# Layer 1 of a two-layer graph network: sums and masks accumulated onto a relu in PSUM, two heads each for VectorE and GpSimd

## The chip, the cores and the metric

The kernel runs on one core of a Trainium2 chip. A core has five engines that work through their own instruction queues and wait for one another by semaphores: TensorE (PE in the profile, with its weight loads as PEld), VectorE (DVE), ScalarE (ACT), GpSimd (POOL) and SyncE (SP), which here only issues DMAs. TensorE writes its results to PSUM, which has eight banks of 128 x 512 float32[...]. The metric is the device time of one execution in microseconds; lower is better.

## The reference

Two layers over 4096 nodes with 512 features. Layer 0 is an attention in which the dense matrix adj is added to the scores. Layer 1, where the change lies, is a graph attention with 8 heads of 64 features. Cut to what matters:

```
h  = relu(layernorm(x))
nX = per-head normalised (h @ W), 8 heads x 64
at1[k,i], at2[k,j] = nX . a1, nX . a2              # per head k
kg[k,i,j] = leaky_relu(at1[k,i] + at2[k,j], 0.2) * adj[i,j]
mg = where(adj[i,j] != 0, kg, -32768)
y  = softmax_j(mg) @ nX + nX
x  = x + elu(y)
```

So each of the 8 x 4096 x 4096 logits is a sum of two vectors, bent at zero, multiplied by adj, masked, and put through an exponential; the row sums of the softmax come out of the product with nX through a column of ones.

## The kernel before

Layer 0 prepares, beside its own work, what layer 1 reads: adj transposed with a tiny value in place of the zeros (gT_d, float32), a mask that is 0 or a huge negative number (nT_d, bfloat16), and the vectors at1 and at2, each split into three bfloat16 parts (z1_d, z2_d), so that a product over six rows gives their exact sum.

Layer 1 is a loop over 512 steps. A step (ic, hg, jt) has 512 target columns (GC), four heads (HG) and 128 source rows. 32 steps (NB, over jt) make a group, which has one pair of accumulators; there are 16 groups, of 8 column chunks with two halves of the heads each. Every instruction goes through seq, so each engine runs its instructions in the order in which the program writes them, which is the order of the loop's body.

With leaky_relu(s) = 0.2 s + 0.8 max(s, 0), the four logits of a step are formed in two ways.

- The left two heads (0 and 1). z_sums makes, on TensorE, 0.2 s in PSUM (line 970, "6*128": a product over six rows) and adds the mask to it with the identity (line 978, eight products of 64 x 64 blocks a step over nb and nx, the mask and its halves swapped). ScalarE's relu (line 986) reads the same PSUM and writes relu(4 z) to SBUF as t; VectorE adds the two (line 1002).
- The right two heads (2 and 3). TensorE makes only at1's part and the mask; VectorE adds the larger of two vectors to it (line 996, one instruction for each head), which is the same function.

Then all four heads are multiplied by adj (g). In an ordinary step VectorE multiplies head 3 from PSUM (line 1001) and GpSimd the other three in SBUF (line 1009, 128x1536). In four "light" steps of each 32 (jt 11, 17, 23, 29) VectorE takes two heads and GpSimd two. ScalarE's exponential (line 1012, 128x2048) and TensorE's product with nX into the accumulators acc (line 1025) follow, three and four steps later.

PSUM has three buffers "d" of two banks, which the left pair, the right pair and small tiles of other work share, and the two accumulators: eight banks. t has six buffers in SBUF. Each step's body issues, in this order: values(n-4), exponent(n-3), leaky(n) with VectorE's work, weigh(n) on GpSimd, z_sums(n+1), relu(n+1). load_adj brings, with SP's queue, the next four steps' masks and g, into two buffers each.

When a group ends, finish spreads its rest over the next 17 steps, by the dictionary later: ScalarE copies the accumulators (copies, line 1041), TensorE turns them (to_rows, line 1047, into a "d" buffer), VectorE divides (lines 1056 and 1057), DMAs on POOL's queue add rows in DRAM (add, line 1063: nX's own rows at step 3, y at 11, x at 14), and ScalarE computes the elu with five kinds of activation (lines 1072 to 1082), before close writes out. The first layer-1 group also runs make_ready for the last rows of layer 0, whose small PSUM tiles use "d".

Of the kernel before, what the change touches and what calls it, by code (L numbers as in the profile page):

```python
# [10 lines left out]
F32 = mybir.dt.float32  # L11
BF16 = mybir.dt.bfloat16
AF = mybir.ActivationFunctionType
# [5 lines left out]
P = 128  # L19
# [59 lines left out]
def fast_path(  # L79
# [817 lines left out]
    with tc.tile_pool(name="ga_in", bufs=2) as inputs, tc.tile_pool(  # L897
# [5 lines left out]
        STEPS = [(ic, hg, jt) for ic in range(NI) for hg in range(NH // HG) for jt in range(NB)]  # L903
        n_steps = len(STEPS)
        inverses = gat.tile([P, NI, 2, 2, 2, 4], F32, name="inverses")
        inverses = gat.tile([P, NI, 2, 2, 2, 4], F32, name="inverses")
        loads, logits, zs, groups = {}, {}, {}, {}

        light = {n for n in range(n_steps) if n % NB in (11, 17, 23, 29)}
        later = {}  # L910

        def load_adj(q):
# [45 lines left out]
                for f in range(2)  # L958
            ]

        def z_sums(n):

            ic, hg, jt = STEPS[n]
            _, masks, z2 = loads[n // JB]
            pair = [None, None]
            for hf in (1, 0):
                pair[hf] = psum.tile([P, 2, GC], F32, name="d", tag="d", bufs=3)
            for hh in (2, 3, 0, 1):
                rows = slice(32 * hh, 32 * hh + 6)
                seq(nc.tensor.matmul(  # L970
                    pair[hh // 2][:, hh % 2, :], z2[rows, ts(jt % JB, P)],
                    groups[ic, hg]["z1"][rows, :], start=True, stop=False,
                ))

            for first in (2, 0):
                for r, c in ((0, 0), (1, 1), (0, 1), (1, 0)):
                    hh, rows = first + r, ts(r, HD)
                    seq(nc.tensor.matmul(  # L978
                        pair[hh // 2][ts(c, HD), hh % 2, :], ident_b[rows, rows],
                        masks[r != c][rows, jt % JB, :], start=False, stop=True,  # L980
                    ))
            zs[n] = pair

        def relu(n):
            t = work.tile([P, HG, GC], F32, name="t", tag="t", bufs=6)
            seq(nc.scalar.activation(t[:, 0:2, :], zs[n][0], AF.Relu, scale=4.0))  # L986
            logits[n] = t

        def leaky(n):

            ic, hg, jt = STEPS[n]
            t, pair, u4 = logits[n], zs.pop(n), groups[ic, hg]["u4"]
            mine = 2 if n in light else 1
            for e in (1, 0):
                h = hg * HG + 2 + e
                seq(nc.vector.scalar_tensor_tensor(  # L996
                    pair[1][:, e, :] if e > 1 - mine else t[:, 2, :], u4[:, e, :],
                    at2m[:, jt, h : h + 1], pair[1][:, e, :], ALU.max, ALU.add,
                ))
            g = loads[n // JB][0][:, jt % JB, :].unsqueeze(1).to_broadcast([P, mine, GC])  # L1000
            seq(nc.vector.tensor_mul(t[:, HG - mine : HG, :], pair[1][:, 2 - mine : 2, :], g))  # L1001
            seq(nc.vector.tensor_add(t[:, 0:2, :], t[:, 0:2, :], pair[0]))  # L1002

        def weigh(n):

            mine = 2 if n in light else 3
            g = loads[n // JB][0][:, STEPS[n][2] % JB, :].unsqueeze(1).to_broadcast([P, mine, GC])
            t = logits[n]
            seq(nc.gpsimd.tensor_mul(t[:, 0:mine, :], t[:, 0:mine, :], g))  # L1009

        def exponent(n):
            seq(nc.scalar.activation(logits[n], logits[n], AF.Exp))  # L1012

        def values(n):

            ic, hg, jt = STEPS[n]
            grp = groups[ic, hg]
            if jt == 0:
                grp["acc"] = [
                    psum.tile([P, GC], F32, name=f"acc{hf}", tag=f"acc{hf}", bufs=1) for hf in range(2)  # L1020
                ]
            t = logits.pop(n)
            for hf in range(2):
                for e in range(2):
                    seq(nc.tensor.matmul(  # L1025
                        grp["acc"][hf][ts(e, HD), :], nX[jt // SB][:, jt % SB, hg * HG + 2 * hf + e, :],
                        t[:, 2 * hf + e, :], start=jt == 0, stop=jt == NB - 1,
                    ))

        def finish(n, ic, hg):  # L1030

# [8 lines left out]
                for hf in range(2):  # L1040
                    seq(nc.scalar.copy(ob[:, hf, :], grp["acc"][hf]))

            def to_rows(hf):
                pt = psum.tile([P, 2, GC], F32, name="pt1", tag="d", bufs=3)
                for b in range(SB):
                    col = (b % 2) * 2 * HB
                    seq(nc.tensor.matmul(  # L1047
                        pt[:, b // 2, col : col + 2 * HB], ob[:, hf, ts(b, P)],
                        back.rearrange("p e c -> p (e c)"), start=True, stop=True,
                    ))  # L1050
                grp["pt"] = pt[:, :, 0 : 4 * HB].rearrange("p k (q c) -> p k q c", c=HB)

            def divide(hf):
                v = grp.pop("pt")
                rinv = inverses[:, ic, hg, hf]
                seq(nc.vector.reciprocal(rinv, v[:, :, :, HD]))
                seq(nc.vector.tensor_mul(  # L1057
                    y[:, hf].rearrange("p (k q) e -> p k q e", k=2), v[:, :, :, 0:HD],
                    rinv.unsqueeze(3).to_broadcast([P, 2, 4, HD]),
                ))  # L1060

            def add(t, what):
                seq(nc.gpsimd.dma_start(out=flat(t), in_=what, accum_op=ALU.add))

            def of_group(ap):
                return ap[ic, hg].rearrange("p f b d -> p (f b d)")

            def flat(t):
                return t.rearrange("p f q e -> p (f q e)")

            def minus(hf):
                seq(nc.scalar.activation(grp["e"][:, hf], y[:, hf], AF.Relu, scale=-1.0))

            def exps(hf):
                e = grp["e"][:, hf]
                seq(nc.scalar.activation(e, e, AF.Exp, scale=-1.0))  # L1076

            def positive():
                seq(nc.scalar.activation(flat(y), flat(y), AF.Relu))  # L1079

            def less_one():
                seq(nc.scalar.add(flat(grp["e"]), flat(grp["e"]), -1.0))

            def close():
                e = grp["e"]
# [5 lines left out]
            if n > n_steps:  # L1091
# [25 lines left out]
                        in_=e[:, hf].rearrange("p (b h) e -> p b (h e)", h=2),  # L1117
                    )
                return
            for d, place, f in (  # L1120
                (0, "mid", copies),
                (1, "mid", lambda: to_rows(0)), (1, "end", lambda: divide(0)),
                (2, "mid", lambda: to_rows(1)), (2, "end", lambda: divide(1)),
                (3, "end", lambda: add(y, of_group(own_d))),
                (6, "end", room), (6, "end", lambda: minus(0)), (7, "end", lambda: minus(1)),
                (8, "end", lambda: exps(0)), (8, "end", positive), (9, "end", lambda: exps(1)),
                (10, "end", less_one), (11, "end", lambda: add(grp["e"], flat(y))),
                (14, "end", lambda: add(grp["e"], of_group(x1_d))), (17, "end", close),
            ):
                later.setdefault((n + d, place), []).append(f)  # L1130

        open_group(0, nc.sync)
        load_adj(0)
# [17 lines left out]
        def at_step(d, f, *a, late=False):  # L1151
            (left_late if late else left).setdefault(1 + d, []).append(lambda: f(*a))

        make_ready(
            NI - 1, last_rows, lambda shape: psum.tile(shape, F32, name="m", tag="d", bufs=3),
            at_step, 4, True,
        )
        z_sums(0)
        relu(0)

        def extra(n, place):
            for f in later.pop((n, place), []):
                f()

        last_in = []
        for n in range(n_steps + 4):
# [15 lines left out]
                    load_features(q)  # L1182
            if n + 10 < n_steps and STEPS[n + 10][2] == 0:
                open_group(n + 10, nc.sync)
            extra(n, "top")
            if 0 <= n - 4 < n_steps:
                values(n - 4)
                if n % JB == 3:
                    loads.pop((n - 4) // JB)
                if STEPS[n - 4][2] == NB - 1:  # L1190
                    finish(n, *STEPS[n - 4][:2])
            if 0 <= n - 3 < n_steps:
                exponent(n - 3)
            extra(n, "mid")
            for f in left.pop(n, []):
                f()
            if n % JB == 2 and n // JB < NS:
                ones_in(n // JB)
            if n < n_steps:
                leaky(n)  # L1200
                weigh(n)
            if n + 1 < n_steps:
                z_sums(n + 1)
                relu(n + 1)
            for f in left_late.pop(n, []):
                f()
            extra(n, "end")
# [10 lines left out]
        nc.vector.tensor_scalar(good[:, 1:2], ends[:, 1:2], 1.0 / TINY, None, ALU.is_le)  # L1218
        nc.vector.tensor_scalar(good[:, 2:3], ends[:, 2:3], HUGE0, None, ALU.is_le)
        nc.vector.tensor_scalar(good[:, 3:4], ends[:, 3:4], 1.0 / HUGE1, None, ALU.is_ge)  # L1220
        pl = psum.tile([4, P], F32, name="pl", tag="d", bufs=3)
        nc.tensor.transpose(pl, good, ident)
        worst = work.tile([4, 1], F32, name="worst", tag="worst", bufs=1)
        nc.vector.tensor_reduce(worst, pl, AX.X, ALU.min)
        pf = psum.tile([1, 4], F32, name="pf", tag="d", bufs=3)
        nc.tensor.transpose(pf, worst, ident[:4, :4])
        every = work.tile([1, 1], F32, name="every", tag="every", bufs=1)
        nc.vector.tensor_reduce(every, pf, AX.X, ALU.min)
# [404 lines left out]
```

## Time and profile before

| | us |
|---|---|
| time, median of 3 runs | 3936.85 (3933.23 to 3938.26) |
| span of the profiled execution | 3931.9 |
| layer 0 and its preparation, in it | 0 to 2095 |
| layer 1, in it | 2095 to 3932 |
| busy in the span: PE, DVE, ACT, POOL | 3693.1, 2873.8, 1778.2, 2498.0 |

The profiled execution is one run with the hardware profiler on; its span, from the first to the last instruction, is 5 us (0.13%) below the median of the plain runs, which include what lies around it. Busy time counts an engine's instructions and not its waits. Over the whole span TensorE is the busiest, but the two layers have different limits, so the shares are to be read by stretch. In a row of the groups the number after the bar is the busy time of all its instructions in us, then the mean of one in ns, then the engine's idle time just before them and who ended it.

### The profile page before, as it was taken

What the parts mean: (1) busy time and instruction counts of PE and PEld (TensorE: products, weight loads), DVE (VectorE), ACT (ScalarE), POOL (GpSimd) and SP (SyncE); (2) the same over time, 40 slices, a digit from 0 to 9 for tenths busy, and PEclk for the clock granted to TensorE, in tenths of its full rate; (3) what the DMA queues carried; (4) which work ended last, traced back from release to release, by engine and by line L of the source; (5) the groups of instructions that cost most, each with busy time, mean ns of one, the idle gap of its engine ahead of it and who ended that gap; (6) DMA issues with size and microseconds to landing.
All of it is one profiled execution on the core that took longest, in us unless ns stands there. A gap on an engine that the chain in (4) does not pass through costs nothing. (4 is left out here: it accounts for less than half of the span.)

```text
span 3931.9 us, 48617 instructions
## 1 busy us (share of the span) xinstructions
PE 3693.1 (94%) x17418; PEld 1719.4 (44%) x17418; DVE 2873.8 (73%) x4307; ACT 1778.2 (45%) x1579; POOL 2498.0 (64%) x1318
## 2 busy tenths in 40 slices
PE   8989999999999999999997899999999999999997
PEld 4446666666666666666663222222222222222222
DVE  5435556565565656556565799999999999999997
ACT  1000011111111111111113688888888888888887
POOL 3432225234252524325255899999999999999997
PEclk9999999999999999999998999999999999999999
DMA  6566766768586676858568776767777777666674
GB/s 202 183 198 191 211 173 197 212 188 213 164 220 184 194 210 184 224 163 216 174 177 171 186 193 182 188 185 193 194 186 190 192 194 189 186 181 187 187 193 128
DMA packets 622634, 745.65 MB, mean 190 GB/s; under 512 B 84656, under 2 KB 467888, under 8 KB 602928
## 3 DMA queue, kind: packets, MB, share of 16 engines
q1 hardware_dynamic: 614512, 717.49, 64.5%
q0 software_dynamic: 6480, 23.60, 3.3%
q8 instruction: 138, 2.26, 0.2%
q10 hardware_dynamic: 1392, 1.38, 0.1%
q14 instruction: 112, 0.92, 0.1%
HBM read 562.23 MB, written 172.23 MB: 187 GB/s over the span
## 5 line engine op out<-in xcount | busy, mean ns | idle before, releaser
L1009 POOL TENSOR_TENSOR t<-t,g 128x1536 f32<-128x1536 f32 (+1 forms) x512 | 1705.9, 3579 | 60.8 <-DVE t L1002 29.9
L1025 PE MATMUL acc<-t,nX 128*64 128x512 f32 x4096 | 999.5, 609 | 50.9 <-ACT t L1012 45.7
L758 POOL TENSOR_TENSOR total<-total,aT 128x512 f32<-128x512 f32 x248 | 340.1, 1371 | 1060.8 <-ACT aT L753 1052.0
L1012 ACT ACTIVATE t<-t 128x2048 f32<-128x2048 f32 x512 | 974.9, 1905 | 1.5 <-POOL t L1009 1.5
L768 PE MATMUL acc<-v,aT 128*128 128x512 f32 x2048 | 961.7, 592 | 0.0
L753 ACT ACTIVATE aT<-aT 128x512 f32<-128x512 f32 x256 | 161.2, 630 | 1323.1 <-DVE aT L748 1301.1
L986 ACT ACTIVATE t<-d 128x1024 f32<-128x1024 f32 x512 | 524.6, 1025 | 287.7 <-PE d L978 287.1
L1002 DVE TENSOR_TENSOR t<-t,d 128x1024 f32<-128x1024 f32 x512 | 619.2, 1209 | 0.1
L768 PEld LDWEIGHTS acc<-v,aT 128*128 128x128 f32 x2048 | 389.2, 190 | 273.1 <-issue 245.1
L1025 PEld LDWEIGHTS acc<-t,nX 128*64 128x64 f32 x4096 | 251.0, 136 | 565.0 <-issue 342.1
L970 PE MATMUL d<-z,z 6*128 6x512 bf16 x2048 | 370.1, 387 | 112.6 <-DVE t L1001 60.4
L996 DVE SCALAR_TENSOR_TENSOR d<-u,at2m,d 128x512 f32<-128x512 f32 x576 | 431.7, 750 | 40.7 <-PE d L978 38.2
L748 DVE TENSOR_TENSOR aT<-aT,X 128x256 f32<-128x256 f32 x512 | 214.6, 419 | 287.9 <-PE X L740 284.8
L1001 DVE TENSOR_TENSOR t<-d,g 128x512 f32<-128x512 f32 (+1 forms) x512 | 384.0, 750 | 15.5 <-DMA g<-gT_d 8.9
L748 DVE TENSOR_TENSOR aT<-aT,Z 128x256 f32<-128x256 f32 x384 | 159.4, 415 | 304.3 <-PE Z L740 299.6
L996 DVE SCALAR_TENSOR_TENSOR t<-u,at2m,d 128x512 f32<-128x512 f32 x448 | 334.6, 747 | 46.5 <-DVE d L996 1.4
L970 PEld LDWEIGHTS <-z 6*128 6x128 bf16 x2048 | 91.4, 91 | 628.3 <-issue 406.6
L978 PE MATMUL d<-nx,ident_b 64*64 64x512 bf16 x2048 | 321.4, 392 | 2.6 <-DMA nx<-nT_d 2.6
L978 PE MATMUL d<-nb,ident_b 64*64 64x512 bf16 x2048 | 321.0, 392 | 0.5 <-DMA nb<-nT_d 0.5
L732 DVE SCALAR_TENSOR_TENSOR gs<-ng,aT 128x512 f32<-128x512 bf16 x256 | 279.4, 1091 | 10.3 <-DMA gT_d<-gs 1.7
L740 PE MATMUL Z<-qt,hS 128*128 128x256 f32 x1024 | 265.5, 382 | 8.3 <-DVE aT L748 8.3
L740 PE MATMUL X<-qt,hT 128*128 128x256 f32 x1024 | 263.6, 380 | 0.5 <-DVE aT L748 0.5
(175 smaller groups left out, 3155.6 us busy)
## 6 DMA issues: line engine op xcount, KB each, us to landing
g<-gT_d SPq DMA_DIRECT2D x128, 1024.0 KB, 5.5
ag<-in_adj_dram SPq DMA_DIRECT2D x256, 256.0 KB, 5.6
hT<-h_d SPq DMA_DIRECT2D x64, 1024.0 KB, 5.9
hS<-s_d SPq DMA_DIRECT2D x64, 1024.0 KB, 8.2
gT_d<-gs SPq DMA_DIRECT2D x256, 256.0 KB, 2.8
nb<-nT_d SPq DMA_DIRECT2D x128, 512.0 KB, 4.4
nx<-nT_d SPq DMA_DIRECT2D x256, 256.0 KB, 5.6
nT_d<-ng SPq DMA_DIRECT2D x256, 128.0 KB, 3.2
```

Of the source, the lines that this page charges most:

```text
L740: seq(nc.tensor.matmul(out, a, b, start=start and k == 0, stop=k == 1, skip_group_check=not start,))
L748: seq(nc.vector.tensor_add(p, p, part))
L768: seq(nc.tensor.matmul(sums[ic][b], probs[s][:, ts(b, P)], v[:, jt, :], start=jt == 0, stop=jt == NB - 1))
L970: seq(nc.tensor.matmul(pair[hh // 2][:, hh % 2, :], z2[rows, ts(jt % JB, P)], groups[ic, hg]["z1"][rows, :], start=True, stop=False,))
L978: seq(nc.tensor.matmul(pair[hh // 2][ts(c, HD), hh % 2, :], ident_b[rows, rows], masks[r != c][rows, jt % JB, :], start=False, stop=True,))
L986: seq(nc.scalar.activation(t[:, 0:2, :], zs[n][0], AF.Relu, scale=4.0))
L996: seq(nc.vector.scalar_tensor_tensor(pair[1][:, e, :] if e > 1 - mine else t[:, 2, :], u4[:, e, :], at2m[:, jt, h : h + 1], pair[1][:, e, ...
L1001: seq(nc.vector.tensor_mul(t[:, HG - mine : HG, :], pair[1][:, 2 - mine : 2, :], g))
L1002: seq(nc.vector.tensor_add(t[:, 0:2, :], t[:, 0:2, :], pair[0]))
L1009: seq(nc.gpsimd.tensor_mul(t[:, 0:mine, :], t[:, 0:mine, :], g))
L1012: seq(nc.scalar.activation(logits[n], logits[n], AF.Exp))
L1025: seq(nc.tensor.matmul(grp["acc"][hf][ts(e, HD), :], nX[jt // SB][:, jt % SB, hg * HG + 2 * hf + e, :], t[:, 2 * hf + e, :], start=jt == 0 ...
```

## The change

In layer 1 each step is made in another way:

- The left sums are made twice. left_sums writes 0.2 s of heads 0 and 1 into a two-bank PSUM tile l, one step ahead; left_relu lets ScalarE write relu(4 z) back over it, in PSUM; sums then adds 0.2 s once more and the mask onto it, on TensorE, with products that continue the accumulation. VectorE's add is gone, and there are two more six-row products a step.
- The right heads get a PSUM bank each (r0 and r1, one buffer each). VectorE's line 1009 writes both to SBUF. GpSimd multiplies these two by g (right_weigh, 128x1024), VectorE the left two from PSUM (left_weigh, 128x1024); there are no light steps any more.
- PSUM: two "l" buffers of two banks, r0, r1 and the two accumulators, in place of three "d". The small tiles of make_ready move to "l".
- The order of the body is now sums(n), left_sums(n+1), VectorE's and GpSimd's work of step n, left_relu(n+1), values(n-4) in two halves, exponent(n-2).
- A group's end: to_rows and divide go through r1 in four steps, one bank each, between the halves of values; the copies stand between the halves of a split exponential. The elu is made with two clamps on GpSimd (negative, positive), two exponentials on ScalarE and two joins on VectorE, and one of the three adding DMAs is gone.

The core of the diff:

```diff
+        def left_sums(n):
+            lefts[n] = psum.tile([P, 2, GC], F32, name="l", tag="l", bufs=2)
+            for hh in range(2):
+                z_product(n, hh, lefts[n][:, hh, :], True, True)
+        def left_relu(n):
+            seq(nc.scalar.activation(lefts[n], lefts[n], AF.Relu, scale=4.0))
+        def sums(n):
+            jt = STEPS[n][2]
+            left = lefts[n]
+            right = [psum.tile([P, GC], F32, name=f"r{e}", tag=f"r{e}", bufs=1) for e in range(2)]
+            out = [left[:, 0, :], left[:, 1, :], right[0], right[1]]
             for hh in (2, 3, 0, 1):
...
+                z_product(n, hh, out[hh], hh > 1)
+            masks = loads[n // JB][1]
             for first in (2, 0):
                 for r, c in ((0, 0), (1, 1), (0, 1), (1, 0)):
...
                     seq(nc.tensor.matmul(
+                        out[first + r][ts(c, HD), :], ident_b[rows, rows],
                         masks[r != c][rows, jt % JB, :], start=False, stop=True,
+                        skip_group_check=first == 0,
                     ))
...
-            g = loads[n // JB][0][:, jt % JB, :].unsqueeze(1).to_broadcast([P, mine, GC])
-            seq(nc.vector.tensor_mul(t[:, HG - mine : HG, :], pair[1][:, 2 - mine : 2, :], g))
-            seq(nc.vector.tensor_add(t[:, 0:2, :], t[:, 0:2, :], pair[0]))
...
+        def right_weigh(n):
             t = logits[n]
-            seq(nc.gpsimd.tensor_mul(t[:, 0:mine, :], t[:, 0:mine, :], g))
+            seq(nc.gpsimd.tensor_mul(t[:, 2:4, :], t[:, 2:4, :], both_heads(n)))
+        def left_weigh(n):
+            seq(nc.vector.tensor_mul(logits[n][:, 0:2, :], lefts.pop(n), both_heads(n)))
...
-                pt = psum.tile([P, 2, GC], F32, name="pt1", tag="d", bufs=3)
-                for b in range(SB):
+            def to_rows(hf, ks=range(2)):
+                if len(ks) == 2:
+                    pt = psum.tile([P, 2, GC], F32, name="pt1", tag="l", bufs=2)
+                else:
+                    pt = psum.tile([P, 1, GC], F32, name="pt1", tag="r1", bufs=1)
...
+            def negative():
+                seq(nc.gpsimd.tensor_scalar(flat(grp["e"]), flat(y), 0.0, LOWEST, ALU.min, ALU.max))
...
             def positive():
+                seq(nc.gpsimd.tensor_scalar(flat(y), flat(y), -LOWEST, 0.0, ALU.min, ALU.max))
...
+            def join(hf):
+                e, z = (t[:, hf].rearrange("p q e -> p (q e)") for t in (grp["e"], y))
+                seq(nc.vector.scalar_tensor_tensor(e, e, -1.0, z, ALU.add, ALU.add))
...
+            for hf in range(2):
+                for k in range(2):
+                    d = 1 + 2 * hf + k
+                    later.setdefault((n + d, "mid"), []).append(
+                        lambda hf=hf, k=k: (to_rows(hf, range(k, k + 1)), divide(hf, range(k, k + 1)))
+                    )
+            for d, f in (
+                (5, lambda: add(y, of_group(own_d))), (8, room), (8, negative), (9, positive),
+                (10, lambda: exp_of(0)), (12, lambda: exp_of(1)),
+                (11, lambda: join(0)), (13, lambda: join(1)),
+                (14, lambda: add(grp["e"], of_group(x1_d))), (17, close),
             ):
...
+            if n < n_steps:
+                sums(n)
             for f in left.pop(n, []):
                 f()
+            if n + 1 < n_steps:
+                left_sums(n + 1)
...
             if n < n_steps:
-                leaky(n)
-                weigh(n)
+                right_leaky(n)
+                right_weigh(n)
+                left_weigh(n)
             if n + 1 < n_steps:
-                z_sums(n + 1)
-                relu(n + 1)
+                left_relu(n + 1)
+            done, ready = 0 <= n - 4 < n_steps, 0 <= n - 2 < n_steps
+            if done:
+                values(n - 4, 0)
+            extra(n, "mid")
+            if done:
+                values(n - 4, 1)
```

## The prediction

> **What bounds the kernel now.** I read four views in this order: the busy shares by stretch, to see which stage the change lies in; the timeline of two steps in that stage, to see which engine never rests; the list of waits there; the groups by line, for prices. (The chain that ended last explains some 5% of the span here, too little to lean on.)
>
> Layer 1 runs from 2095 us to the end at 3932 us. The copies at line 1041 close each of its 16 groups of 32 steps; they start at 2271.41, 2383.43, ... 2713.43, 2822.86, 2932.66, 3042.10, ... 3913.80 us. From the first to the last that is 1642.4 us for 15 groups: **109.5 us a group, 3.42 us a step**. Two whole groups, as stretches (busy us of PE, PEld, DVE, ACT, POOL with counts, granted clock, DMA share, GB/s):
>
> ```profile
> 2713.43:2822.86 109.43, 101.28 (x660) 27.90 (x656) 105.02 (x133) 94.75 (x73) 108.96 (x36) 1.00 0.70 189
> 2932.66:3042.10 109.44, 101.22 (x660) 27.91 (x656) 105.03 (x133) 94.78 (x73) 107.77 (x36) 1.00 0.71 189
> ```
>
> GpSimd (POOL) is busy 98 to 99% and VectorE (DVE) 96%. The timeline (start, duration, engine, line) shows both in one ordinary step and the start of a "light" one, where VectorE takes a second head:
>
> ```profile
> 3105.20 0.75 DVE L996 SCALAR_TENSOR_TENSOR d<-u,at2m,d 128x512 f32<-128x512 f32 x1
> 3105.27 1.02 ACT L986 ACTIVATE t<-d 128x1024 f32<-128x1024 f32 x1 [0.41 <-PE d L978]
> ...
> 3106.06 0.75 DVE L996 SCALAR_TENSOR_TENSOR t<-u,at2m,d 128x512 f32<-128x512 f32 x1
> 3106.19 1.91 ACT L1012 ACTIVATE t<-t 128x2048 f32<-128x2048 f32 x1
> ...
> 3106.72 0.68 DVE L1001 TENSOR_TENSOR t<-d,g 128x512 f32<-128x512 f32 x1
> ...
> 3106.96 0.89 PE L970 MATMUL d<-z,z 6*128 6x512 bf16 x4
> 3107.32 1.21 DVE L1002 TENSOR_TENSOR t<-t,d 128x1024 f32<-128x1024 f32 x1
> 3107.46 0.10 PEld L970 LDWEIGHTS <-z 6*128 6x128 bf16 x2 [0.41 <-DVE t L1001]
> 3107.78 0.40 PE L978 MATMUL d<-nb,ident_b 64*64 64x512 bf16 x2
> ...
> 3108.34 1.94 PE L1025 MATMUL acc<-t,nX 128*64 128x512 f32 x8
> 3108.45 1.54 DVE L996 SCALAR_TENSOR_TENSOR d<-u,at2m,d 128x512 f32<-128x512 f32 x2
> 3108.54 1.02 ACT L986 ACTIVATE t<-d 128x1024 f32<-128x1024 f32 x1 [0.45 <-PE d L978]
> ...
> 3110.09 1.23 DVE L1001 TENSOR_TENSOR t<-d,g 128x1024 f32<-128x1024 f32 x1
> 3111.24 1.21 DVE L1002 TENSOR_TENSOR t<-t,d 128x1024 f32<-128x1024 f32 x1
> ```
>
> VectorE starts one instruction as the last ends: 3105.20 to 3108.45, **3.25 us an ordinary step**, and 3108.45 to 3112.36, 3.91 us a light one. 28 x 3.25 + 4 x 3.91 = 106.6 of the 109.5 us; the rest is the group's end. TensorE waits for VectorE (line 970 above, 0.41 us) and ScalarE for TensorE. GpSimd fits exactly: 28 multiplies of 3.4 us (one that follows idle time, at 2226.11 us, took 3.42; the 3707 ns of the row below count time in which the one before still ran), 4 of 2.4 and three DMA issues of 1 us are about 108. So VectorE and GpSimd bind together; the prices come from these groups:
>
> ```profile
> L1009 POOL TENSOR_TENSOR t<-t,g 128x1536 f32<-128x1536 f32 x448 | 1566.6, 3707 | 60.4 <-DVE t L1002 29.7 <-DMA nX<-nX_d 22.4 <-DVE nX L1145 7.9
> L1002 DVE TENSOR_TENSOR t<-t,d 128x1024 f32<-128x1024 f32 x512 | 619.2, 1209 | 0.1
> L732 DVE SCALAR_TENSOR_TENSOR gs<-ng,aT x256: 691/693/1727, 277.6 to 2065.2; 128x512 f32<-128x512 bf16 x128
> ```
>
> **What the Trainium skill says.** "TensorEngine Tiling (Array Packing)", Key Properties: changing the tiling mode drains TensorE. The trace agrees: two sets of 64x64 products follow each other in 0.23 us (3107.78, 3108.02), but from the 6-row products to the first set it is 0.32 and from the second set to line 1025 it is 0.32, some 0.1 us for each change of shape. "SBUF — State Buffer", SBUF: two separate sides: a VectorE operation with two SBUF inputs and a GpSimd operation that reads SBUF exclude each other for a whole instruction. Line 732, the only frequent one of that kind, agrees: 691 ns alone, up to 1727. "PSUM — Partial Sum Buffer", Specifications: ScalarE writes faster to PSUM than to SBUF; no run here shows a relu within PSUM.
>
> **The change, part by part.** Per step, start to start:
>
> - *VectorE* loses the add (line 1002, 3108.45 - 3107.32 = 1.13) and its mask multiply of one head (0.60), and gets one of two heads straight from PSUM (the light form of line 1001: 3111.24 - 3110.09 = 1.15). With two line 996 operations (0.75 each) that is 2.65 us, for 3.25 and 3.91.
> - *GpSimd* multiplies two heads: the only unhurried 128x1024 of line 1009 (at 2364.33 us) took 2.39, for 3.4. The group then needs 32 x 2.39 = 76.5, two DMA issues 2.2, and two new clamps of 128x1024, whose kind the trace lacks: from 0.9 (less than the 2.39 over two inputs, by far) to 1.7 (twice line 756's copy of 512, 847 ns); I take 1.7. Sum 82: covered by TensorE's step.
> - *ScalarE* keeps 0.92 + 1.80 = 2.72. The relu now stays in PSUM: bounds 0.85 (the skill's "faster") and 1.1; I take 0.92, since line 996 shows 750 ns into PSUM and 747 into SBUF. Four activations at a group's end become two (-2.1 us), and one exponential is split around the copies (+0.15).
> - *TensorE* gets two 6-row products a step, as the left sums are made twice, first alone for the relu and then on top of it. Now unhindered: 0.32 (four 6-row) + 0.55 (eight masks) + 1.87 (values; 3105.09 to 3106.95) = 2.74. The added pair comes after the masks and before the values, two changes of shape more: 0.31, as for the four, which run side by side. It could cost 0.21 (one stream, nothing drained) or 0.47 (a wait in its midst). **3.05 us a step.**
>
> So TensorE becomes the bound. Does a wait stretch that? From a step's first product at 0: right masks done 0.72, VectorE's two operations 0.8 to 2.3, left multiply to 3.45; left sums of the next step at 0.87, done 1.26, relu 1.38 to 2.4, exponential to 4.1. TensorE's new wait for the relu comes due at 3.15 (0.6 spare; behind it would queue masks and values, and VectorE's next step). Its wait for a free "l" buffer at 0.87 needs the left multiply before, done at 0.4 + 0.1 (0.3 spare; behind it the values). ScalarE has 0.33 spare, VectorE 0.4. All hold.
>
> The group's end, over 32 x 3.05 = 97.6:
> - to_rows now goes through "r1", the single buffer of head 3, in four steps. TensorE: 0.55 (half of the 1.09 now) + 0.15 for splitting the values. But the next step's product into r1 waits for divide, which stands behind the left multiply: 3.45 + 0.2 + 0.42 (half of line 1057's 691 ns, rounded up) + 0.1 = 4.15 instead of 3.05. Four times 1.1 = 4.4.
> - join, on VectorE, has two SBUF inputs (0.68 as line 1111). GpSimd's multiply runs 2.35 to 4.7, so by the lock join starts at 4.7 rather than 3.45, ends at 5.4, and the next step's operations come 1.5 late; after VectorE's slack the step after next is some 1.1 late. Twice: 2.2 (0 without the lock).
> - Copies between the halves of an exponential: relu 0.9 late against 0.6 spare, 0.3. exp_of twice 0.53: within ScalarE's slack.
> - SP's loads stand at the same steps and the multiply that frees a "g" buffer lags less, so it is asked for earlier; 5.5 us to land against four steps, 12.2 us: hidden. On POOL's queue the own_d add moves from step 3 to 5 with three steps (9.2 us) to its reader against 5.6 to land: hidden; the add of y goes.
>
> Sum: 97.6 + 4.4 + 2.2 + 0.3 = 104.5 a group, 5.0 less; fifteen times 75 us. The first group (2095 to 2271 us) is slowed by layer 0's last rows, whose 13 small tiles move to the two "l" buffers: each makes the next left sums wait for the left multiply, 1 to 1.5 us more, while other steps gain as above. I take 0, from -15 to +15. The end after 3913.8 is the same code. The profiled span is 3931.9 us, 5 below the median of 3936.85 shown; that goes on top: 3931.9 - 75 + 5 = **3862 us**.
>
> **Rivals.**
> - *TensorE is cheaper than I think, and join isn't held.* The pair costs 0.21: 32 x 2.95 + 4.7 = 99.1, 10.4 less, 156 in all: 3781. For it: tiles run side by side. Against: the 0.32 at each change of shape.
> - *Slower: the ring through the two "l" buffers binds.* Left multiply to left sums two steps on, values, products, masks, two VectorE operations, left multiply: 0.1 + 0.31 + 1.87 + 0.32 + 0.47 + 1.5 + 1.15 + 0.1 = 5.8 us for two steps, 2.9 each. It decides from (109.5 - 6.9) / 32 = 3.2 a step, a ring of 6.4: 0.6 more, as with VectorE's operations at 0.86 (the spacing now after a line 996 into PSUM) and 1.22 and hops of 0.2. At 3.3 the group is 112.5, 45 us more: 3982. Against it: both operations now write SBUF, after which the spacing is 0.66.
> - *No change.* The group's ends cost 5 us more than worked out, the four r1 waits and two joins chaining into later steps: 3937.
>
> **How the numbers follow.** Steps at 3.05: 0.62, with 3862; cheaper TensorE 0.18; no change 0.05; the ring 0.15. About 0.2%, 8 us, is what a measurement of this kernel can tell from no change. Faster 0.80, same 0.05, slower 0.15. The range leaves out the far side of the ring and the last of the cheap case: 3785 to 3945.
>
> **What would show it.** Right: ordinary steps at about 3.05 us with TensorE unbroken; VectorE and GpSimd idle 0.3 to 0.7 each; a stretch of four longer steps (4.1) after each copy; joins longer than 0.68. Wrong: left products (line 965) waiting for VectorE, ordinary steps above 3.2, or a relu much over 1.02 us.

## Result: the steps are as fast as forecast, and SP's queue takes most of it back

| | before | after |
|---|---|---|
| time, median of 10 runs each, us | 3936.99 (3932.41 to 3945.42) | 3924.44 (3918.11 to 3928.28) |
| span of the profiled execution, us | 3931.9 | 3922.2 |
| ratio after to before | | 0.9966, 95% interval 0.9957 to 0.9975 |

The changed kernel is 12.5 us faster; the forecast was 75 us faster (3862 us, from 3785 to 3945). The copies (now line 1050) start at 2269.20, 2378.17, ... 2712.86, 2822.26, 2933.58, 3043.11, ... 3905.57 us: from the first to the last (3905.57 - 2269.20) / 15 = **109.1 us a group**, against 109.5 before and 104.5 in the forecast. The same two whole groups as before, in the windows view (busy us of PE, PEld, DVE, ACT, POOL with counts, granted clock, DMA share, GB/s):

```profile
2712.86:2822.26 109.40, 104.61 (x724) 29.13 (x720) 87.06 (x107) 92.27 (x71) 79.59 (x37) 0.98 0.70 184
2933.58:3043.11 109.53, 105.68 (x724) 29.22 (x720) 87.06 (x107) 92.26 (x70) 79.59 (x37) 0.97 0.68 184
```

VectorE fell from 105 to 87 us and GpSimd from 109 to 80, TensorE rose from 101 to 105, and yet the group takes as long. TensorE is busy for 96% and not for 100%, and its granted clock is below 1.00. One ordinary step of the changed kernel in the timeline (start, duration, engine, line; some lines are left out here and in the timelines below):

```profile
2844.26 0.39 PE L965 MATMUL r<-z,z 6*128 6x512 bf16 x2
2844.58 0.40 PE L991 MATMUL r<-nb,ident_b 64*64 64x512 bf16 x2
2844.82 0.38 PE L991 MATMUL l<-nb,ident_b 64*64 64x512 bf16 x2
2845.14 1.41 DVE L1009 SCALAR_TENSOR_TENSOR t<-u,at2m,r 128x512 f32<-128x512 f32 x2 [0.53 <-PE r L991]
2845.14 0.39 PE L965 MATMUL l<-z,z 6*128 6x512 bf16 x2
2845.46 1.94 PE L1034 MATMUL acc<-t,nX 128*64 128x512 f32 x8
2845.57 1.01 ACT L977 ACTIVATE l<-l 128x1024 f32<-128x1024 f32 x1 [0.25 <-PE l L965]
2846.46 1.22 DVE L1018 TENSOR_TENSOR t<-l,g 128x1024 f32<-128x1024 f32 x1
2846.49 1.90 ACT L1022 ACTIVATE t<-t 128x2048 f32<-128x2048 f32 x1
2846.72 2.38 POOL L1015 TENSOR_TENSOR t<-t,g 128x1024 f32<-128x1024 f32 x1 [0.46 <-ACT l L977]
2847.33 0.39 PE L965 MATMUL r<-z,z 6*128 6x512 bf16 x2
```

From 2844.26 to 2847.33 the step takes **3.07 us**; TensorE starts its four sums, the masks (0.32 later), the left pair (0.56), the values (0.32) and the next step without a gap. VectorE and GpSimd now have idle time. So the ordinary step is what was forecast (3.05). The steps of the group from 2822.26 to 2933.58, taken between the starts of the relu (line 977), show where the rest is: most are 3.07; those after the copies 3.77, 3.34, 4.00, 4.00 and 3.93; those with the joins 3.92 and 3.84; and steps 24 and 25 are **8.52 and 5.38 us**, 7.8 more than two ordinary ones. Some other groups lose less and some more. There, in the timeline:

```profile
2888.86 0.39 PE L965 MATMUL r<-z,z 6*128 6x512 bf16 x2
2890.58 0.40 PE L991 MATMUL r<-nb,ident_b 64*64 64x512 bf16 x2 [1.32 <-DMA nb<-nT_d]
2892.60 0.37 PE L991 MATMUL r<-nx,ident_b 64*64 64x512 bf16 x1 [1.62 <-DMA nx<-nT_d]
2894.04 0.58 PE L991 MATMUL r<-nx,ident_b 64*64 64x512 bf16 x1 [1.07 <-DMA nx<-nT_d]
2894.05 1.00 PE L991 MATMUL l<-nx,ident_b 64*64 64x512 bf16 x2
2895.51 3.68 PE L1034 MATMUL acc<-t,nX 128*64 128x512 f32 x8
2899.13 0.61 PE L965 MATMUL r<-z,z 6*128 6x512 bf16 x2
2900.90 1.94 PE L1034 MATMUL acc<-t,nX 128*64 128x512 f32 x8
```

TensorE waits for the masks, 4.0 us in three pieces, and then works at half speed: its granted clock is 0.50 from 2893.61 to 2900.43 us, and the values take 3.68 us instead of 1.94. By the starts of the sums, step 24 takes 10.27 us (2888.86 to 2899.13) and the next 3.64: of the 7.8 us too many 4.0 are waiting, and the other 3.8 go with the slower clock (6.4 us of work at half speed lose 3.2). The masks are late because of SP. Its issues around that place in the changed kernel (start, duration, line, what is loaded):

```profile
2865.79 0.36 SPq L928 DMA_DIRECT2D g<-gT_d  x1
2877.92 1.51 SPq L1108 DMA_DIRECT2D out_dram<-e  x2
2879.48 0.50 SPq L941 DMA_DIRECT2D z<-z_d  x1
2880.07 0.40 SPq L913 DMA_DIRECT2D z<-z_d  x1
2880.52 0.44 SPq L944 DMA_DIRECT2D u<-u_d  x1
2881.05 0.46 SPq L917 DMA_DIRECT2D nb<-nT_d  x1
2881.61 2.68 SPq L923 DMA_DIRECT2D nx<-nT_d  x2
2884.39 0.55 SPq L928 DMA_DIRECT2D g<-gT_d  x1
2884.98 0.77 SPq L944 DMA_DIRECT2D u<-u_d  x1
```

Line 1108 is close, which writes the finished group out; lines 913 to 928 are the load for steps 24 to 27 (z2, nb, nx, g); lines 941 and 944 are z1 and u of the next group. In the kernel before, the load's four parts came first and then close (line 1087 there), z1 and u:

```profile
2875.66 0.34 SPq L915 DMA_DIRECT2D z<-z_d  x1
2876.21 0.36 SPq L919 DMA_DIRECT2D nb<-nT_d  x1
2883.62 0.36 SPq L930 DMA_DIRECT2D g<-gT_d  x1
2884.09 1.00 SPq L1087 DMA_DIRECT2D out_dram<-e  x2
```

In the changed kernel close stands ahead of the load. It waits for the adding DMA of x1_d (issued on POOL's queue at 2872.6 us), so SP stands still until 2877.92; behind it z1 and half of u are mixed into the load. The waits view of SP, from 2300 to 3900 us (waited for: us in all, times, longest), before had 1.6 us there and now has

```profile
SPq L1108 <- DMA e<-x_d: 174.8, 15, 11.8
```

which is 11.7 us a group, and TensorE's waits on DMA, which the kernel before didn't have in this stretch, are

```profile
PE r L991 <- DMA nx<-nT_d: 29.4, 28, 1.7
PE r L991 <- DMA nb<-nT_d: 18.2, 14, 1.8
```

The diff doesn't touch close. But close is the one part of a group's work that doesn't go through seq, so the program's text doesn't fix the place of its two DMAs among SP's others. What moved it, and z1 and half of u with it, is not shown; when close is fixed behind the load, z1 and u stand behind the load again too (e1). The description of the kernel before, "every instruction goes through seq", is wrong in this one place.

### The profile page after: what moved, and what is told of

The parts are those of the page before. It is cut to its first block, busy times and chain, and to the rows that moved or that the text cites. A ratio compares the mean times of both kernels' runs of the same rounds, so it can differ in the third digit from the quotient of the medians.

```text
span 3922.2 us, 51218 instructions
## 1 busy us (share of the span) xinstructions
PE 3751.8 (96%) x18442; PEld 1739.8 (44%) x18442; DVE 2580.9 (66%) x3885; ACT 1740.7 (44%) x1534; POOL 2041.9 (52%) x1333
## 3 DMA queue, kind: packets, MB, share of 16 engines
q8 instruction: 146, 2.39, 0.3%
## 5 line engine op out<-in xcount | busy, mean ns | idle before, releaser
L1015 POOL TENSOR_TENSOR t<-t,g 128x1024 f32<-128x1024 f32 x512 | 1221.7, 2387 | 505.6 <-ACT l L977 291.0
L1022 ACT ACTIVATE t<-t 128x2048 f32<-128x2048 f32 (+1 forms) x527 | 977.0, 1854 | 0.2 <-POOL t L1015 0.2
L1009 DVE SCALAR_TENSOR_TENSOR t<-u,at2m,r 128x512 f32<-128x512 f32 x1024 | 719.1, 743 | 375.4 <-issue 223.8
L977 ACT ACTIVATE l<-l 128x1024 f32<-128x1024 f32 x512 | 516.6, 1009 | 305.2 <-PE l L965 300.2
L1018 DVE TENSOR_TENSOR t<-l,g 128x1024 f32<-128x1024 f32 x512 | 623.2, 1217 | 20.0 <-DMA g<-gT_d 16.3
L965 PE MATMUL l<-z,z 6*128 6x512 bf16 x2048 | 403.2, 390 | 31.2 <-DVE t L1018 10.6
L740 PE MATMUL X<-qt,hS 128*128 128x256 f32 x1024 | 263.9, 380 | 0.0
L740 PEld LDWEIGHTS Z<-qt,hS 128*128 128x128 f32 x1024 | 192.9, 191 | 131.9 <-issue 56.9
L991 PE MATMUL r<-nx,ident_b 64*64 64x512 bf16 x1024 | 214.9, 404 | 30.0 <-DMA nx<-nT_d 29.9
L740 PEld LDWEIGHTS X<-qt,hT 128*128 128x128 f32 x1024 | 195.0, 191 | 81.8 <-issue 55.0
```

The lines of the kernel that those rows point to most:

```text
L740: seq(nc.tensor.matmul(out, a, b, start=start and k == 0, stop=k == 1, skip_group_check=not start,))
L965: seq(nc.tensor.matmul(out, loads[n // JB][2][rows, ts(jt % JB, P)], groups[ic, hg]["z1"][rows, :], start=start, stop=stop, skip_group_che ...
L977: seq(nc.scalar.activation(lefts[n], lefts[n], AF.Relu, scale=4.0))
L991: seq(nc.tensor.matmul(out[first + r][ts(c, HD), :], ident_b[rows, rows], masks[r != c][rows, jt % JB, :], start=False, stop=True, skip_gr ...
L1009: seq(nc.vector.scalar_tensor_tensor(t[:, 2 + e, :], u4[:, e, :], at2m[:, jt, h : h + 1], right[e], ALU.max, ALU.add))
L1015: seq(nc.gpsimd.tensor_mul(t[:, 2:4, :], t[:, 2:4, :], both_heads(n)))
```

## Experiments

In all of them the group time is (start of the last copies - start of the first) / 15, from the trace.

### e1: close fixed behind the load

```diff
-                    nc.sync.dma_start(
+                    seq(nc.sync.dma_start(
                         out=ap, in_=e[:, f].rearrange("p (b h) e -> p b (h e)", h=2)
-                    )
+                    ))
```

> Only the place of close's two DMAs on SP's queue is changed: pinned behind the load for steps 24 to 27, as in the kernel before. Theory A (SP's queue order: close waits at the head of SP's queue for the adding DMA of x1_d, and the masks behind it come late): the stall of 7.8 us at steps 24 and 25 goes, a group takes 103 to 104.5 us, TensorE no longer waits for nb and nx, and the time is 3830 to 3860 us. Rival B (the group's end moves too much by DMA at once, whatever the order): TensorE still waits for nb or nx, the group stays at 109 us, 3915 to 3930 us. Rival C (TensorE's pauses are hidden by something else that is just as late, such as VectorE or GpSimd): the waits for nb and nx go but others come, 3890 us or more.

Measured 3837.12 us, ratio to before 0.9739 (0.9723 to 0.9755): **87 us faster than the changed kernel by one word on two DMAs**. A group takes 103.4 us. The windows view of one group:

```profile
2687.37:2790.91 103.54, 102.21 (x724) 28.57 (x720) 86.95 (x107) 92.26 (x71) 79.52 (x37) 1.00 0.73 195
```

The counts and the busy time of VectorE, ScalarE and GpSimd are the changed kernel's; TensorE's busy time is 3 us less at a clock of 1.00, and it is busy for 99%. Its waits for nb and nx are gone. SP's order in one group, in the timeline:

```profile
2946.16 0.34 SPq L913 DMA_DIRECT2D z<-z_d  x1
2946.70 0.47 SPq L917 DMA_DIRECT2D nb<-nT_d  x1
2947.26 1.36 SPq L923 DMA_DIRECT2D nx<-nT_d  x2
2950.57 0.36 SPq L928 DMA_DIRECT2D g<-gT_d  x1
2951.03 1.00 SPq L1108 DMA_DIRECT2D out_dram<-e  x2
2952.08 1.43 SPq L941 DMA_DIRECT2D z<-z_d  x1
2953.56 3.41 SPq L944 DMA_DIRECT2D u<-u_d  x2
```

Theory A holds and B and C fall: nothing else was as late. (The mean of 103.4 us holds one group of 106.94 us and a short last one; most groups take 103.55.) What stayed open is which part of the other order does the harm, close's wait or the data that is queued with it.

### e2: the kernel before, with close ahead of the load

```diff
-                (14, "end", lambda: add(grp["e"], of_group(x1_d))), (17, "end", close),
+                (14, "end", lambda: add(grp["e"], of_group(x1_d))), (17, "head", close),
...
+            extra(n, "head")
             if n % JB == (2 if q == NS - 1 else 0) and q < n_steps // JB:
                 load_adj(q)
```

(close's DMAs go through seq here too.)

> The kernel before with close's two DMAs put ahead of the load for steps 24 to 27 on SP's queue, nothing else. In its trace the adding DMA issued at 2875.5 us lands some 7.9 us later, so the masks, issued at 2876.2 us there, would be issued at about 2886 us and land 4.4 to 6 us later, where the first sums of step 24 come at about 2892 us. Theory A: the order alone costs time in the kernel before too, by 0 to 4 us a group, since its steps are longer and leave more room than in the changed kernel: 3937 to 4000 us, likeliest 3960, with waits of TensorE for nb or nx in the trace that it hadn't. Rival B (the order is harmless): 3937 us within 8, and no such waits.

Measured 3942.68 us, ratio 1.0006 (0.9997 to 1.0015): no difference: within the 8 us of rival B, at the lowest edge of what theory A allowed and far from the 3960 called likeliest. Yet SP did stand still, as long as in the changed kernel:

```profile
SPq L1087 <- DMA e<-x_d: 151.3, 14, 11.7
```

(waits of SP from 2300 to 3800 us), while TensorE waited for nx for 1.4 us in all, and not for nb. So in this kernel the order is harmless, as B has it, and close's wait at the head of SP's queue isn't enough by itself. That might have come from the longer steps before, or from z1 and u, which here stand behind the load. e5 and e9 separate these.

### e5, e6 and e9: close, and z1 and u, ahead of the load, each alone and both

All three start from e1. e5 has close ahead of the load, z1 and u behind it. e6 has z1 and u ahead of the load, close behind it. e9 has close, then z1 and u, then the load.

```diff
+            extra(n, "head")                                     # e5, e9: close
+            if n + 12 < n_steps and STEPS[n + 12][2] == 0:       # e6, e9: z1, u
+                open_group(n + 12, nc.sync)
             if n % JB == (2 if q == NS - 1 else 0) and q < n_steps // JB:
                 load_adj(q)
...
-            if n + 10 < n_steps and STEPS[n + 10][2] == 0:       # e6, e9
-                open_group(n + 10, nc.sync)
```

> The changed kernel with close pinned ahead of the load for steps 24 to 27 and the next group's z1 and u behind that load: the order of e2, with the changed kernel's steps. It splits the cause of the stall in two. If close's wait alone makes it (SP stands until 2877.9 us, masks then issued some 8.8 us before their first use, behind 512 KB of close): a stall of 3 us or more a group stays, 3880 us or more. If it takes z1 and u in between the parts of the load as well (they put 640 KB more ahead of and among the masks): at most 2 us a group, 3837 to 3870 us, likeliest 3850.

> e1 with the next group's z1 and u issued ahead of the load for steps 24 to 27, two steps earlier than now, and close behind the load as in e1. If what is issued amid the load matters by itself: the masks are issued near 2874 us where 2889 us is in time, so even with 640 KB ahead of them they land in time: 3837 us within 8. If the amount of data ahead of the masks is what delays them whatever the time of issue: 2 us or more a group, 3867 us or more.

> e5 with one thing moved: z1 and u of the next group stand between close and the load for steps 24 to 27, so all of it is released when close's wait ends and 768 KB more than close's are queued ahead of the masks. e5 had SP's full wait (178 us, 11.9 a group) and lost almost nothing. If it takes both, the wait and that data ahead of the masks, to make TensorE late: 4 to 8 us a group more than e5, 3900 to 3960 us, with waits for nb and nx. If z1 and u don't matter: e5's 3846 us, plus some 10 us once, which e6 showed for the first group when z1 and u are asked for two steps earlier there.

In the table, the issue of nb and the landing of the masks (nb first, the second half of nx last) are medians over the 14 groups that have such a load, in us after the group's copies. The masks are first used at 66.9 us where nothing is late (e1).

| ahead of the load for steps 24 to 27 | SP waits in close | nb issued | masks land | time, us | ratio to before (95%) | group, us |
|---|---|---|---|---|---|---|
| nothing (e1) | no | 52.2 | 58.8 to 61.3 | 3837.12 | 0.9739 (0.9723 to 0.9755) | 103.4 |
| z1, u (e6) | no | 52.2 | 58.8 to 61.4 | 3844.62 | 0.9756 (0.9739 to 0.9772) | 103.1 |
| close (e5) | yes | 57.5 | 62.9 to 65.4 | 3846.07 | 0.9764 (0.9748 to 0.9781) | 103.4 |
| close, then z1, u mixed into the load (the changed kernel) | yes | 58.4 | 68.3 to 71.2 | 3924.44 | 0.9966 (0.9957 to 0.9975) | 109.1 |
| close, z1, u (e9) | yes | 59.2 | 70.4 to 73.5 | 3968.15 | 1.0069 (1.0049 to 1.0089) | 111.3 |

e6 costs the groups nothing: its time lies ahead of its first copies, which start at 2280.39 us and not at 2269.76 (why is not shown). But e6 doesn't have z1 and u waiting in front of the masks. Without close's wait SP issues them 8 us before the load, and they have landed, 52.0 us after the copies, when nb is issued. So no run has this data directly ahead of the masks without the wait; what e6 shows is that its place in the order alone does no harm.

In e5 close's wait delays the masks, and they still land 1.5 us before their use. Its groups of 103.4 us are those of its fastest execution (3839.31 us), so in the median one the wait may cost up to half a us a group. In e9 close's wait holds z1 and u back as well and releases all of it at once, right ahead of the masks: 111.3 - 103.4 = 7.9 us a group more than e5. Its time lies 8 us above the expected range, and its first copies start late as in e6, at 2282.39 us. e9's SP, in the timeline,

```profile
2899.11 1.58 SPq L1108 DMA_DIRECT2D out_dram<-e  x2
2900.74 0.50 SPq L941 DMA_DIRECT2D z<-z_d  x1
2901.28 1.10 SPq L944 DMA_DIRECT2D u<-u_d  x2
2902.48 0.45 SPq L913 DMA_DIRECT2D z<-z_d  x1
2903.03 0.49 SPq L917 DMA_DIRECT2D nb<-nT_d  x1
```

and what TensorE does next:

```profile
2911.68 0.61 PE L965 MATMUL l<-z,z 6*128 6x512 bf16 x2 [3.67 <-DMA z<-z_d]
```

show it: SP issues the whole row within some 5 us, so the parts of the load are only some 2 us later on SP than in e5, but 512 KB of close, 128 of z1 and 512 of u are queued ahead of z2, which lands after 9 us instead of the usual 2.1. I had expected TensorE's waits at nb and nx (and have 8.9 us of them, for nx); most are at z2 (46 us from 2300 to 3800 us), which the left sums need one step earlier than the masks. The Trainium skill, "DMA: Bandwidth & Descriptors", Queues, rings and completion order, says that the DMAs that SP issues share one ring on each DMA engine, taken in order. The traces agree: in the changed kernel's group shown above, everything from close to the last u lands in the order in which SP issued it, and nx of this load takes 5.4 to 8.6 us to land in e5, 9.9 to 12.3 in the changed kernel, where z1 and half of u stand ahead of it too, and 11.9 to 13.8 in e9.

That e2 lost nothing and e5 hardly anything, with the same order but different steps, says that the longer steps of before were not needed to hide close's wait: z1 and u behind the load were enough. No run puts all of it ahead of the load in the kernel before.

### e3 and e4: what binds the step

e3 issues left_sums' pair twice; e4 gives VectorE a memset of 128x256 behind each left multiply. Both start from e1.

```diff
-            for hh in range(2):
+            for hh in (0, 1, 0, 1):                              # e3
                 z_product(n, hh, lefts[n][:, hh, :], True, True)
...
                 left_weigh(n)
+                seq(nc.vector.memset(spare, 0.0))                # e4
```

> e1 with left_sums' two products issued twice over (the second pair writes the same values again): two more six-row products a step. If TensorE is the bound of every step, the time rises against e1 by 0.21 us (one more stream of 512 columns at the trace's spacing, nothing drained) to 0.31 us a step, 512 steps: 107 to 159 us. If another engine or the ring through the l buffers sets the step: less than 30 us.

> e1 with a memset of 128x256 float32 in SBUF behind the left multiply of every step on VectorE, 0.1 to 0.35 us (bounded by its other instructions of 256 to 512 elements). If TensorE binds and VectorE has some 0.4 us a step to spare: within 10 us of e1. If VectorE or the ring through its left multiply sets the step: the memset's length times 512, 50 to 180 us more.

e3 took 3920.16 us, 83 more than e1. Its ordinary steps are 3.28 us, exactly the 0.21 more of one stream (2845.31 to 2848.59 us between two steps' sums); over 512 steps that would be 107 us. The missing 24 us are in the group's ends: a group takes 5.2 us more and not 6.7, as TensorE had waits there to fill: those for VectorE at r0 and r1, 15.1 us from 2300 to 3800 us in e1, are 0.4 in e3. So TensorE sets every ordinary step. The first pair cost 0.32 us and a second one in the same shape 0.21: the difference fits one more change of shape at the 0.1 us that the prediction read from the trace before.

e4 took 3854.47 us, 17 more than e1 (between its two expectations, close to the first), for 512 memsets of 0.27 us (139 us of VectorE's time). The ordinary step stays at 3.07; the 0.9 us a group come where VectorE is already late, after the copies and at the joins. VectorE has some 0.5 us of room in an ordinary step (0.53 us idle in the changed kernel's step above, 0.25 us in e4's) and none in those.

### e7: divide ahead of the left multiply

```diff
                 right_weigh(n)
-                left_weigh(n)
...
             extra(n, "mid")
+            if n < n_steps:
+                left_weigh(n)
             if done:
                 values(n - 4, 1)
```

> e1 with VectorE's left multiply put behind divide in the four steps that turn the accumulators (elsewhere VectorE's order is the same). The prediction held that these steps are long because r1 waits for divide behind the left multiply: then they fall from 4.0 us towards 3.1, and the group gets 2 to 4 us shorter, 3780 to 3807 us. But e1's trace shows TensorE nearly unbroken in them (0.32 + 0.56 + 0.31 + 1.01 + 0.65 + 1.01 = 3.86 us of its own by the starts, 0.14 us of waiting): then 0.5 us a group, 3829 us, from 3820 to 3845.

Measured 3829.90 us, ratio 0.9722 (0.9706 to 0.9738), 7 us less than e1: the second expectation, not the prediction's. The three steps of 4.00, 4.00 and 3.93 us become 3.91 each. These steps are long because TensorE turns the accumulators between two halves of the values; the wait for r1 adds 0.1 us to them. It ends close behind TensorE's own work, so e4's memset, which delays divide, makes each of them 0.22 us longer.

### e8, e10 and e11: join off VectorE, and everything together

```diff
-                seq(nc.vector.scalar_tensor_tensor(e, e, -1.0, z, ALU.add, ALU.add))
+                seq(nc.gpsimd.tensor_add(e, e, z))
...
-                seq(nc.gpsimd.tensor_scalar(flat(y), flat(y), -LOWEST, 0.0, ALU.min, ALU.max))
+                seq(nc.gpsimd.tensor_scalar(flat(y), flat(y), 0.0, -1.0, ALU.max, ALU.add))
...
-                (14, lambda: add(grp["e"], of_group(x1_d))), (17, close),
+                (14, lambda: add(grp["e"], of_group(x1_d))), (21, close),      # e10, e11
```

e8 has the first two edits on e1, e10 all three, e11 those and e7's.

> e1 with join's addition on GpSimd (the -1 goes into the positive clamp, which loses its bound against huge values), so that VectorE no longer has an instruction with two inputs in SBUF in layer 1. If VectorE's join, held for 2.08 us instead of 0.68, makes the two longer steps (4.20 and 3.84 us against 3.07): 1.9 us a group less, 3808 us, from 3800 to 3820. If GpSimd, which would have two instructions of about 1.2 us more a group and 0.7 us a step to spare, becomes late: no gain, 3830 us or more.

> e8 with close four steps later, behind the load for steps 28 to 31. In e8 the two join steps had fallen from 4.20 and 3.84 us to 3.24 and 3.07 us, but the adding DMA came later on POOL's queue, close waited for it (38.8 us in all) and two steps of 4.21 and 4.68 us followed. If that wait of SP is where e8's gain went: 1.9 us a group less than e1, 3808 us, from 3800 to 3818, without waits for nx. If GpSimd's additions cost it in another way: 3830 us or more.

> e10 with e7's order (divide ahead of the left multiply): the version that the experiments point to. e7 took 0.35 us a group off e1, e10 should take 1.9: together 3800 us, from 3792 to 3812. If the two get in each other's way (GpSimd and VectorE later in the steps after the copies): no better than the better of the two alone.

e8 took 3853.87 us, 17 more than e1, though the joins' steps fell to TensorE's pace (3.24, 2.90, 3.24, 2.90 and 3.07 us, where e1 has 3.24, 2.90, 3.92, 3.08 and 3.84; the 4.20 of the expectation is one group's). The adding DMA comes later on POOL's queue, so close waits again, now ahead of the load for steps 28 to 31 (38.8 us in 15 waits), and long steps follow in nearly every group (4.21 and 4.68 us in one), with z1 and u between close and the load as in e9. In e10, with close behind that load, they are gone: 3810.26 us, ratio 0.9673 (0.9655 to 0.9692), 1.9 us a group less than e1, or 1.6 from one of e1's common groups of 103.55 us to e10's of 101.93. e11 took **3806.51 us, ratio 0.9663 (0.9646 to 0.968)**, the fastest version: 118 us less than the changed kernel. In its trace TensorE is busy from the first copies to the last (windows view):

```profile
2269.00:3790.00 1521.00, 1521.00 (x10766) 422.98 (x10764) 1246.25 (x1552) 1378.46 (x1032) 1270.34 (x576) 1.00 0.71 197
```

What is left above 32 x 3.07 = 98.2 us a group is for the most part the turning of the accumulators, TensorE's own work.

## Why the prediction was right and wrong

- **The step that failed: "SP's loads stand at the same steps".** It took the order of SP's queue from the program's text, and the text doesn't fix it for close. The load for steps 24 to 27 stood behind close's wait of 11.7 us a group and behind close's and z1's data and a part of u's, so that the masks landed at 68.3 to 71.2 us instead of 58.8 to 61.3 and were due at 66.9. This costs 7.8 us in the group that was taken apart, where the sum had 0, and 109.1 - 103.4 = 5.7 us in the mean group, 86 us over the fifteen. TensorE's 47.6 us of waits for masks and 68.2 us at half clock from 2300 to 3900 us, of which half is lost, make 82 of these 86 us. The same sentence worked out g's landing against its lead (hidden) but not that of the masks, and it counted nothing that SP issues beside the load. With that one order put right (e1), the kernel takes 3837 us, 25 us less than the forecast, some 16 of them from groups of 103.4 instead of 104.5 us.
- **TensorE's step, 3.05 us: right.** 3.07 in the trace; e3 shows that nothing else sets it. The new pair at 0.31 measured 0.32. So the rival of the cheaper TensorE falls.
- **The ring through the l buffers: not there.** TensorE's wait for a free l buffer is 5.9 us over fifteen groups (row below); VectorE's line 1009 takes 743 ns apiece with its output in SBUF, as assumed.
- **The relu in PSUM, 0.92 us from start to start: right** (2845.57 to 2846.49). The Trainium skill's statement that ScalarE writes faster to PSUM ("PSUM — Partial Sum Buffer", Specifications) agrees, by little: 1009 ns a relu, against 1025 before.
- **GpSimd: covered, as said.** The multiply takes 2.39 us, as forecast; the clamps take 1.04 and 1.03 us, where 1.7 was taken (bounds 0.9 to 1.7).
- **The four turning steps, 4.4 us: too large, and for the most part from another cause.** They cost 3.0 us over ordinary ones (0.27 + 0.93 + 0.93 + 0.86). The forecast had 0.7 us of TensorE's own work in each and let a longer wait for r1 set their 4.15 us; in fact its own work there makes 0.32 + 0.56 + 0.31 + 1.01 + 0.65 + 1.01 = 3.86 us, the wait adds 0.14, and e7 gains only 0.1 us a step.
- **The joins, 2.2 us by the shared port: right in kind.** They took 2.08 us in every group (0.68 before); the ten from 2526 to 2980 us all began while a GpSimd multiply ran and ended 0.54 to 0.55 us after its end, so they were held until then. They cost 0.85 + 0.77 = 1.6 us; without them, e10's steps there are ordinary ones. e10 takes the whole join off VectorE, not the port's wait alone, so the share of the port in the 1.6 us wasn't measured by itself; of an unheld join's 0.68 us, some 0.5 would fit into VectorE's room.
- **The first group, 0 us: right.** Its copies start at 2269.20 instead of 2271.41 us. **The copies, 0.3 us:** 0.7.
- Ordinary steps, turning, joins and copies as measured make 98.2 + 3.0 + 1.6 + 0.7 = 103.5 us a group, where 104.5 was forecast and e1 has 103.4. The rival "no change" came near in time (3937), but by a mechanism that isn't there: the steps behind the turning and the joins are ordinary ones again, so the group's ends don't chain.

The rows of the changed kernel from 2300 to 3900 us (busy us, mean ns of one, idle before and who ended it):

```profile
L1015 POOL TENSOR_TENSOR t<-t,g 128x1024 f32<-128x1024 f32 x468 | 1117.6, 2388 | 429.9 <-ACT l L977 277.0 <-DVE t L1009 78.0 <-DMA g<-gT_d 62.8
L977 ACT ACTIVATE l<-l 128x1024 f32<-128x1024 f32 x466 | 470.2, 1009 | 252.8 <-PE l L965 251.9
L965 PE MATMUL l<-z,z 6*128 6x512 bf16 x1866 | 365.0, 388 | 5.9 <-DVE t L1018 5.9
L1103 DVE SCALAR_TENSOR_TENSOR e<-e,y 128x512 f32<-128x512 f32 x30 | 62.3, 2076 | 0.0
L1095 POOL TENSOR_SCALAR y<-y 128x1024 f32<-128x1024 f32 x15 | 15.5, 1034 | 0.0
```

The reader sees in the first row that GpSimd, once busy for 98 to 99% of a group, now waits, and for g (62.8 us) only because g stands in the same late load.

## What to carry to other kernels

When a change makes a kernel's steps shorter, follow every queue that issues loads across the whole period, with all that it issues: one issue that waits, and the data queued between it and the load, can cost most of what the steps have gained. An instruction without a fixed place in an otherwise fixed order is a place where an edit elsewhere can move it, so read the order of the built kernel, not that of the text. A stall that recurs at one step of a period is found quickest by listing the step lengths of one period and then what TensorE waits for in the longest.

## What was not expected of the hardware

- In the group shown TensorE waited for 4.0 us in three pieces and then had a granted clock of 0.50 for 6.8 us: 3.68 us instead of 1.94 for the values, which nearly doubled the price of the stall. From 2300 to 3900 us the changed kernel has 14 such stretches, all of 3.41 us or a multiple of it, ten of them of 3.41; the kernel before has two, and e5 has none between its first copies and its last. The Trainium skill, "TensorE: Matmul & The Clock Gate", Part 1: The HAM clock gate, says that the clock halves after an idle window of about 3.4 us. The length of the stretches agrees. But the time before them was not idle: in the 3.41 us ahead of each, TensorE was busy for 0.8 to 1.9 us (0.78 from 2890.20 to 2893.61), so a few short waits close together are enough.
- GpSimd's clamp by minimum and maximum of 128x1024 float32 took 1.03 us; the same shape with a maximum and an addition took 3.63 us in e10, row of the POOL groups from 2300 to 3800 us:

```profile
L1095 POOL TENSOR_SCALAR y<-y 128x1024 f32<-128x1024 f32 x15 | 54.4, 3629 | 1.3
```

- A delay costs nothing until the lead is used up: close's wait puts off the masks' landing by some 4 us in e5 and leaves 1.5 us, with GpSimd's waits for g at 10.0 us in all; z1 and u ahead of the masks put it off by 8 us more in e9.
